# Sending the keys of a linear attention through a DRAM scratch and turning them in 32x32 blocks on VectorE

## The chip, the cores and the metric

The kernel runs on one core of a Trainium2 chip. The metric is the device time of one execution in microseconds, the median over several runs; less is better. Engine names are those of the profile: PE is TensorE (PEld its weight loads), DVE is VectorE, ACT is ScalarE, POOL is GpSimd, SP is SyncE, which here issues nearly all DMAs.

## The reference, cut to what matters

Input `x` is 16 images of 56 x 56 tokens with 128 channels, float32. Layer 0 is a group norm and shifted window attention with 4 heads over windows of 7 x 7 tokens, added to `x`. Layer 1 reads each image as 3136 tokens in order:

```
t = t + L1_attn(ln(t))    # causal linear attention, below
t = t + L1_ffn(ln(t))     # batch-normed projection, then a recurrence over all tokens

def L1_attn(x, W, b):                      # per image
    q, k, v = split(x @ W.T + b)
    q = elu(q) + 1;  k = elu(k) + 1
    num[t] = q[t] @ sum_{s <= t} outer(k[s], v[s])
    den[t] = q[t] . sum_{s <= t} k[s] + 1e-6
    return num / den
```

The change concerns `k = elu(k) + 1`, which the kernel calls the keys' features.

## The kernel before

All arithmetic is float32. An image's tokens are cut into six full groups of 512 tokens (four chunks of 128) and one short group of 64 tokens. A window row is 56 tokens x 7 rows, eight per image.

**The plan.** The work up to the recurrence is not written in program order. Every piece is a `plan.step(engine, cost, rank, emit, after, takes, drops, lag)`: its engine, how long it holds the engine, a due time, the function that issues it, the steps that must come first, the buffers it takes and those it drops, and after how long its result is there. `Plan.emit` runs a list schedule over all steps with these costs, repeats it forwards and backwards 200 times, keeps the shortest plan, and issues all steps in the order of their planned starts. So on each engine the order of instructions is fixed when the kernel is built. SP is planned like an engine: its steps are DMA issues, and it takes them in that order. The instructions that belong together of two images overlap in this order: while the window rows of one image are worked on, the token groups of the image before it are.

**A window row** (`window_row`): projections of queries and keys (L857) and values (L878) on PE, scores (L902), masking and maxima on DVE (L913, L925), subtraction on POOL (L928), exponential on ACT (L938), sums on DVE (L942), scaling on POOL (L947), a PE transpose (L957), and the mix with the values (L976), copied out by ACT.

**A token group** (`token_group`): output projection (L1224), added on DVE (L1233); statistics on DVE (L1080), the rest of the norm on POOL; the normalised tokens are turned so that channels lie on partitions (`xnT`). From `xnT` come two features, `feature(1)` for the keys (tile `f1`) and `feature(0)` for the queries (tile `f0`): a projection on PE (L1259), two activations on ACT (L1269, L1278) and a maximum on DVE (`larger`, L1287). Values come from L1312 and L1321. The products of keys and queries inside a chunk (L1375) are masked on DVE (L1385, tile `A`). `attend` adds up state times queries (L1404) and `A` times values (L1407); `gather` adds keys times values to the running state in `state_bank` (L1415), which ACT copies out per chunk (L1427). `gather` wants the keys with tokens on partitions (tile `k`), while `f1` has channels on partitions. DVE divides and updates the tokens (L1477, L1480, L1484), SP stores them to `x_d` (L1184), and a second norm and projection (L1502) gives the inputs of the recurrence (`staged`, stored by L1537, once per image).

**How something is turned.** There are two ways. On PE: four transposes of 128 x 128 into a PSUM bank and a copy by ACT; the keys take this way in all groups (`turn_k`, L1335, and `k_out`, L1339). Through DRAM (`through_dram`): SP stores the tile to a scratch (`away`, L1050), then issues four reads of 64 KB (`back`, L1057), which bring the 32-row blocks to the partitions where they belong, and one DVE instruction transposes within 32 x 32 blocks (L1129). The normalised tokens of both norms (keys `"a"` and `"f"` of `xn_d`) take this way in the full groups of images 0 to 14, as `blocks_moved` says; the last image and the short groups use PE. Four slots (`xp`) hold what is read back, three (`xm`) what is sent; `f1`, `f0`, `r`, `A` have one buffer each, `k` has two, PSUM has three banks (`b`) for everything but scores and states.

**DMA around it.** Besides, SP loads the tokens of later images by group (L323), loads each image a second time in 128-byte runs for the window attention (`load_blocks`, L335, turned by DVE in L676), and stores groups and staged inputs. All of these stand in one in-order queue.

After the plan comes the recurrence over the tokens, cut into segments (L1785, L1788, L1773, L1822, L1831), which the change does not touch.

Of the kernel before, what the change touches and what calls it, by code (L numbers as in the profile page):

```python
# [26 lines left out]


TOL2 = 2.0 ** -38
KEYS = ('f', 'a')  # L30


class Buf:
# [201 lines left out]
def tile_conv_attn_hybrid(  # L235
# [19 lines left out]
    nc = tc.nc  # L255
# [6 lines left out]
    G = 4  # L262
# [27 lines left out]
    xn_d = {  # L290
        key: dram.tile([B - 1, NG - 1, 4, P, P], F32, name=f"xn{key}_d") for key in KEYS
    }
# [65 lines left out]
    def flat(to):  # L358

        dims = " ".join("abc"[: len(to.shape) - 1])  # L360
        return to.rearrange(f"p {dims} -> p ({dims})")
# [66 lines left out]
    with ExitStack() as s1:  # L428
# [14 lines left out]
        def own(buf, *shape):  # L443

            key = buf.tag, buf.place
            if key not in owned:
                owned[key] = keep.tile(list(shape), F32, name=f"{buf.tag}_{buf.place}")
            return owned[key]
# [3 lines left out]
        def at_spare(buf):  # L452

            k = AT_SPARE[buf.tag] + buf.place
            return flat(spare[1])[:, GT * k : GT * (k + 1)]
# [109 lines left out]
        s = issued = plan.step("SP", 0.1, -1.0, lambda: None, lag=19.0)  # L565
# [80 lines left out]
        def part(g, full, mini):  # L646

            return full if g < NG - 1 else mini
# [392 lines left out]
        def blocks_moved(key, b, g):  # L1041

            return key in KEYS and b < B - 1 and g < NG - 1

        def through_dram(key, b, g, src, xp, rank, after, drops):

            there = xn_d[key][b, g]

            def away():
                nc.sync.dma_start(  # L1050
                    there.rearrange("s p r -> p s r"),
                    src().rearrange("p (s r) -> p s r", s=4),
                )

            def back():
                for s4 in range(4):
                    nc.sync.dma_start(  # L1057
                        at_spare(xp)[32 * s4 : 32 * (s4 + 1)].rearrange(
                            "i (q r) -> i q r", q=4
                        ),  # L1060
                        there[s4].rearrange("(q i) r -> i q r", q=4),
                    )

            s = plan.step("SP", 0.7, rank, away, after, drops=drops, lag=2.6)
            return plan.step("SP", 1.6, rank, back, [s], takes=[xp], lag=3.6)

        def layer_scale(t, g, d, key, rank, after, to, drops=()):
# [79 lines left out]
            if blocks:  # L1147
                s = through_dram(key, t["b"], g, lambda: d["xm"], xp, rank, [sc], [xn])
                s = plan.step(
                    "DVE",  # L1150
                    (0.59, 0.68),
                    rank,
                    turn_blocks,
                    [s, chain[key]],
                    takes=[to],
                    drops=[xp],
                )
                chain[key] = s
                return s, sc
# [40 lines left out]
        def token_group(b, g, i, t, turned_x, rows_done, oT_buf, xt_buf, rank):  # L1200


            n = f"{b}_{g}"
            d, df = {}, {}
# [3 lines left out]
            nt = t1 - t0  # L1208
# [38 lines left out]
            s = st("DVE", part(g, (0.61, 0.69), (0.20, 0.28)), rank, plus_attention, [s0, s1], drops=[bo])  # L1247
# [5 lines left out]
            def feature(j):  # L1253
                key = f"f{j}"
                bp, r, f = Buf("b"), Buf("r"), Buf(key)

                def proj():
                    d[f"p{j}"] = bank(bp, P, nt)
                    nc.tensor.matmul(  # L1259
                        d[f"p{j}"],  # L1260
                        awc_sb[:, j * P : (j + 1) * P],
                        d["xT"][:, :nt],
                        start=True,
                        stop=True,
                    )

                def relu():
                    d[f"r{j}"] = own(r, P, GT)[:, :nt]
                    nc.scalar.activation(  # L1269
                        d[f"r{j}"],  # L1270
                        d[f"p{j}"],
                        AF.Relu,
                        bias=bqk_neg[:, j : j + 1],
                        scale=-1.0,
                    )

                def expo():
                    nc.scalar.activation(d[f"r{j}"], d[f"r{j}"], AF.Exp, scale=-1.0)  # L1278

                def larger():  # L1280
                    d[key] = own(f, P, GT)
                    to, a1, a2 = d[key][:, :nt], d[f"p{j}"], d[f"r{j}"]
                    if j and blocks_moved("k", b, g):
                        to = to.rearrange("p (c k) -> p k c", k=G)
                        a1 = a1.rearrange("p (k c) -> p k c", k=G)
                        a2 = a2.rearrange("p (k c) -> p k c", k=G)
                    nc.vector.scalar_tensor_tensor(  # L1287
                        to,
                        a1,
                        bqk_one[:, j : j + 1],  # L1290
                        a2,
                        ALU.add,
                        ALU.max,
                    )

                p = st("PE", part(g, (0.86, 1.02), (0.17, 0.33)), rank, proj, [xo, *first], takes=[bp], drops=[xnT])
                s = st("ACT", part(g, (0.58, 0.69), (0.22, 0.31)), rank, relu, [p], takes=[r])
                s = st("ACT", part(g, (0.53, 0.63), (0.16, 0.26)), rank, expo, [s])
                return st("DVE", part(g, (0.65, 0.74), (0.18, 0.27)), rank, larger, [s], takes=[f], drops=[r, bp]), f

            first = [] if b else [made["awc"], made["bqk"], made["fwTc"]]
# [3 lines left out]
            def chunk(f, cc):  # L1305
                return f[:, CK * cc : CK * (cc + 1)]
# [22 lines left out]
            s = st("PE", part(g, (0.89, 1.05), (0.22, 0.38)), rank, values, [xo, *first, *last_pd[i % 2]], takes=[bv], drops=[xnT])  # L1329
# [10 lines left out]

            def turn_blocks():
                d["k"] = own(k, P, G, C)
                nc.vector.transpose(
                    d["k"].rearrange("p k (q c) -> p k q c", q=4),
                    at_spare(xp).rearrange("p (q c k) -> p k q c", q=4, k=G),
                )

            def keys(cc):
                if blocks_moved("k", b, g):
                    return d["f1"].rearrange("p (c k) -> p k c", k=G)[:, cc]  # L1350
                return chunk(d["f1"], cc)

            bk, k, bA, A = Buf("b"), Buf("k"), Buf("b"), Buf("A")
            if blocks_moved("k", b, g):
                xp = Buf("xp")
                s = through_dram("k", b, g, lambda: d["f1"], xp, rank, [fk], [bfk])
                ko = st(
                    "DVE",
                    (0.59, 0.68),
                    rank,  # L1360
                    turn_blocks,
                    [s, chain["k"]],
                    takes=[k],
                    drops=[xp],
                )
                chain["k"] = ko
            elif g < NG - 1:
                s = st("PE", (0.44, 0.61), rank, turn_k, [fk], takes=[bk], drops=[bfk])
                ko = st("ACT", (0.48, 0.59), rank, k_out, [s], takes=[k], drops=[bk])


            def products():
                d["pA"] = bank(bA, P, nk, np)
                for cc in range(nk):
                    nc.tensor.matmul(  # L1375
                        d["pA"][:, cc, :],
                        keys(cc),
                        chunk(d["f0"], cc)[:, :np],
                        start=True,
                        stop=True,  # L1380
                    )

            def A_out():
# [6 lines left out]
                )  # L1390

            s = st("PE", part(g, (0.89, 1.05), (0.13, 0.29)), rank, products, [fq, fk], takes=[bA], drops=[bfk])
            Ao = st("DVE", part(g, (0.60, 0.69), (0.13, 0.22)), rank, A_out, [s], takes=[A], drops=[bA])

# [98 lines left out]
            s = st("DVE", (0.29, 0.37), rank, divisors, pns)  # L1493
# [4 lines left out]
            s, scaled = layer_scale(t, g, df, "f", rank, [up], xfT, [xt_buf])  # L1498
# [24 lines left out]
            s = st("PE", part(g, (0.86, 1.02), (0.17, 0.33)), rank, whole, [s], takes=[bw], drops=[xfT])  # L1523
# [192 lines left out]
    with ExitStack() as s2:  # L1716
# [177 lines left out]
        d = ryo.tile([P, 2, B, SEG], F32, tag="y", name="seam")[:, 0, :, 0 : SEG - 1]  # L1894
# [95 lines left out]
```

## Time and profile before

| | before |
|---|---|
| median of 3 runs | 1694.72 us (1693.42 to 1697.08) |
| the profiled execution | 1699.48 us, span 1697.7 us |
| granted TensorE clock, mean | 0.992 |
| first to fifteenth store of staged inputs | 174.2 to 1480.6 us |
| HBM read, written | 147.94 MB, 122.65 MB |
| DMA queue that SP issues to | 537232 packets, 269.89 MB, 54.5% of 16 engines |

The profile shows one execution. A row of a group names line, engine, operation, output and inputs, shape and count, then total busy time, the mean of one in ns, and the engine's idle time just before with what ended it. The names in a row are the program's: tiles that lie in the buffer `spare` (all `xm` and `xp` slots do) are shown as `spare`; `xna_d` and `xnf_d` are the scratches of the two norms. A weight load and a matmul are recorded apart (PEld, PE), and a float32 matmul shows as two records. In a window row the columns are the stretch, its length, busy us with counts of PE, PEld, DVE, ACT and POOL, the granted clock, the DMA engines' busy share and GB/s.

### The profile page before, as it was taken

The page shows a single profiled execution, that of the slowest core. Times are in us where ns is not written, and L with a number is a line of the kernel's source. Part 1 is how long each engine was busy: PE and PEld are TensorE (multiplying, and loading weights), DVE is VectorE, ACT ScalarE, POOL GpSimd, SP SyncE. Part 2 cuts the span into 40 slices and gives each one's busy share as a digit, 9 for nine tenths or more (in the row PEclk, how much of TensorE's full clock was granted, in tenths as well). Part 3 has the DMA queues.
Part 4 walks back from the last instruction along what each step waited for, and adds up shares of the span by engine and source line. Part 5 has one row for each costly group of instructions (what it writes and reads, how often), then busy time and mean ns, then how long its engine had stood idle before and what let it go on. Part 6 is the DMA issues. An engine that isn't in the chain of part 4 may idle for free.

```text
span 1697.7 us, 63511 instructions
## 1 busy us (share of the span) xinstructions
PE 1651.5 (97%) x25819; PEld 1348.0 (79%) x25819; DVE 1444.7 (85%) x3354; ACT 1139.0 (67%) x2846; POOL 1152.5 (68%) x2042
## 2 busy tenths in 40 slices
PE   7999999999999999999999999999999998999997
PEld 6778878888887888888888888888787887786875
DVE  5889988898979898988988898989788876777997
ACT  5667667667676676766766767667666675666765
POOL 6788778688778687877876887787676765651000
PEclk9999999999999999999999999999999999999998
DMA  5465646364545547463746365545543343558999
GB/s 134 102 161 122 173 126 170 103 163 135 154 132 139 129 119 186 116 167 107 182 116 159 114 141 157 151 124 131 143 121 96 102 140 95 163 175 325 405 418 378
DMA packets 539117, 274.81 MB, mean 162 GB/s; under 512 B 208960, under 2 KB 522560, under 8 KB 537024
## 3 DMA queue, kind: packets, MB, share of 16 engines
q1 hardware_dynamic: 537232, 269.89, 54.5%
q8 instruction: 204, 3.34, 0.8%
q10 hardware_dynamic: 1584, 0.79, 0.2%
q14 instruction: 97, 0.79, 0.1%
HBM read 147.94 MB, written 122.65 MB: 159 GB/s over the span
## 4 chain that ended last, share of the span: by engine, by line
PE 81%; DVE 7%; POOL 4%; DMA 3%; issue 3%; SPq 1%; ACT 1%; DVEq 0%; POOLq 0%; ACTq 0%
PE bank L1259 9%; PE bank L857 9%; PE bank L878 6%; PE pair L902 6%; PE pair L957 5%; PE state_bank L1415 5%; PE pair L1404 5%; PE pair L1407 5%; PE pair L976 5%; PE bank L1312 5%; PE bank L1375 5%; PE bank L1224 5%; PE bank L1502 4%; DVE z_buf L1773 3%; PE z_buf L1785 3%
## 5 line engine op out<-in xcount | busy, mean ns | idle before, releaser
L928 POOL TENSOR_TENSOR s<-s,mx 128x784 f32<-128x784 f32 x128 | 192.4, 1503 | 84.9 <-DVE mx L925 82.3
L947 POOL TENSOR_TENSOR p_buf<-p_buf,rc 128x784 f32<-128x784 f32 x128 | 194.6, 1521 | 80.4 <-DVE rc L944 39.7
L1259 PE MATMUL bank<-xnT,awc_sb 128*128 128x512 f32 (+1 forms) x448 | 211.2, 554 | 4.6 <-DVE xt_buf L1233 3.4
L1269 ACT ACTIVATE r<-bank,bqk_neg 128x512 f32<-128x512 f32 (+1 forms) x224 | 142.7, 637 | 101.0 <-PE bank L1259 84.6
L1404 PEld LDWEIGHTS pair<-state,f 128*128 128x128 f32 x768 | 126.1, 191 | 53.5 <-issue 35.9
L1287 DVE SCALAR_TENSOR_TENSOR f<-bank,bqk_one,r 128x512 f32<-128x512 f32 (+1 forms) x224 | 147.6, 659 | 23.2 <-ACT r L1278 10.7
L1407 PE MATMUL pair<-v_buf,A 128*128 128x129 f32 x800 | 155.4, 276 | 0.8 <-issue 0.4
L967 ACT COPY pT<-pair 128x904 f32<-128x904 f32 x128 | 118.1, 923 | 54.6 <-PE pair L957 42.4
L1415 PEld LDWEIGHTS state_bank<-v_buf,k 128*128 128x128 f32 x768 | 123.7, 192 | 38.9 <-issue 21.0
L1415 PE MATMUL state_bank<-v_buf,k 128*128 128x129 f32 x768 | 153.8, 282 | 0.5 <-ACT state L1427 0.2
L1427 ACT COPY state<-state_bank 128x129 f32<-128x129 f32 x384 | 105.2, 274 | 72.7 <-PE state_bank L1415 69.9
L1404 PE MATMUL pair<-state,f 128*128 128x129 f32 x768 | 152.1, 280 | 0.0
L913 DVE TENSOR_TENSOR s<-pair,wmask_sb 128x784 f32<-128x784 f32 x128 | 122.9, 960 | 32.0 <-PE pair L902 27.8
L942 DVE TENSOR_REDUCE sm<-p_buf 128x16 f32<-128x784 f32 x128 | 121.9, 952 | 21.3 <-ACT p_buf L938 21.1
L1213 POOL TENSOR_TENSOR xt_buf<-xt_buf,bout_sb 128x512 f32<-128x512 f32 (+1 forms) x112 | 129.3, 1159 | 14.2 <-DMA xt_buf<-in_x_dram 13.9
L1788 ACT ACTIVATE y_a<-z_buf,bsh 128x256 f32<-128x256 f32 (+1 forms) x218 | 103.3, 474 | 45.5 <-PE z_buf L1785 41.5
L1278 ACT ACTIVATE r<-r 128x512 f32<-128x512 f32 (+1 forms) x224 | 130.7, 584 | 2.5
L902 PEld LDWEIGHTS pair<-kT,q_buf 32*49 32x49 f32 x8192 | 106.3, 121 | 32.3 <-issue 16.3
L1785 PE MATMUL z_buf<-y_a,fvT_sb 128*128 128x256 f32 (+1 forms) x432 | 129.7, 385 | 0.5 <-ACT y_a L1788 0.4
L902 PE MATMUL pair<-kT,q_buf 32*49 32x49 f32 x8192 | 122.6, 206 | 4.8 <-issue 4.8
L957 PEld LDWEIGHTS pair<-ident,p_buf 113*128 113x128 f32 x1024 | 108.1, 142 | 21.6 <-issue 9.6
L1407 PEld LDWEIGHTS pair<-v_buf,A 128*128 128x128 f32 x800 | 121.8, 192 | 3.9 <-issue 1.9
(162 smaller groups left out, 4619.0 us busy)
## 6 DMA issues: line engine op xcount, KB each, us to landing
x_d<-xt_buf SPq DMA_DIRECT2D x96, 256.0 KB, 2.5
xt_buf<-in_x_dram SPq DMA_DIRECT2D x93, 256.0 KB, 3.4
spare<-in_x_dram SPq DMA_DIRECT2D x60, 392.0 KB, 4.7
xs_d<-staged SPq DMA_DIRECT2D x15, 1568.0 KB, 7.0
xna_d<-spare SPq DMA_DIRECT2D x90, 256.0 KB, 2.5
spare<-xna_d SPq DMA_DIRECT2D x360, 64.0 KB, 2.0
xnf_d<-spare SPq DMA_DIRECT2D x90, 256.0 KB, 2.3
spare<-xnf_d SPq DMA_DIRECT2D x360, 64.0 KB, 2.1
```

Source lines behind the costliest of these rows:

```text
L857: nc.tensor.matmul(d[key], wqkv_sb[:, j * P : (j + 1) * P], xk, start=True, stop=True)
L902: nc.tensor.matmul(sc[64 * hh : 64 * hh + WT, hp, w * WT : (w + 1) * WT], qT[r : r + HD, w * WT : (w + 1) * WT], d["kT"][r : r + HD, w * W ...
L928: nc.gpsimd.tensor_tensor(d["sf"], d["sf"], d["mx"].unsqueeze(2).to_broadcast([P, nb, WT]), ALU.subtract,)
L947: nc.gpsimd.tensor_tensor(prf, prf, d["rc"].unsqueeze(2).to_broadcast([P, nb, WT]), ALU.mult)
L957: nc.tensor.transpose(pt[:, hp, w2, 0:NQ2], pr[0:NQ2, hp, 2 * w2 : 2 * w2 + 2, :].rearrange("p w k -> p (w k)"), ident[0:NQ2, 0:NQ2],)
L1259: nc.tensor.matmul(d[f"p{j}"], awc_sb[:, j * P : (j + 1) * P], d["xT"][:, :nt], start=True, stop=True,)
L1269: nc.scalar.activation(d[f"r{j}"], d[f"p{j}"], AF.Relu, bias=bqk_neg[:, j : j + 1], scale=-1.0,)
L1287: nc.vector.scalar_tensor_tensor(to, a1, bqk_one[:, j : j + 1], a2, ALU.add, ALU.max,)
L1404: nc.tensor.matmul(to, chunk(d["f0"], cc), t["states"][c], start=True, stop=False)
L1407: nc.tensor.matmul(to, d["A"][:, cc, :], v1[:, cc, :], start=c == 0, stop=True)
L1415: nc.tensor.matmul(t["pd"], d["k"][:, cc, :], v1[:, cc, :], start=c == 0, stop=True, skip_group_check=True,)
L1785: nc.tensor.matmul(z, fvT_sb, y_prev, start=False, stop=True, skip_group_check=True)
```

## The change

The keys join the tiles that go through DRAM: in the full groups of images 0 to 14, `f1` is stored to a scratch of its own, `xnk_d`, read back, and turned by DVE into `k`; `turn_k` and `k_out` stay for the last image. The way back differs from that of the norms. For the norms, POOL has already written its output with channels interleaved, and each of the four reads has four runs of 512 bytes per partition. `f1` is stored as it is, so each read picks, for each of 32 partitions, 16 runs of 32 elements (128 bytes). The planned costs of the two SP steps are those of the norms. A branch in `larger` and a helper `keys`, which interleaved the key features for such a way and were not entered before (`"k"` was not in `KEYS`), are taken out.

```diff
-KEYS = ('f', 'a')
+KEYS = ('f', 'a', 'k')
...
         def through_dram(key, b, g, src, xp, rank, after, drops):
             there = xn_d[key][b, g]
+            runs = there.rearrange("s (q i) r -> i (s q) r", q=4)
...
             def back():
                 for s4 in range(4):
-                    nc.sync.dma_start(
-                        at_spare(xp)[32 * s4 : 32 * (s4 + 1)].rearrange(
-                            "i (q r) -> i q r", q=4
-                        ),
-                        there[s4].rearrange("(q i) r -> i q r", q=4),
-                    )
+                    to = at_spare(xp)[32 * s4 : 32 * (s4 + 1)]
+                    if key == "k":
+                        to = to.rearrange("i (n c) -> i n c", c=32)
+                        part = runs[:, :, 32 * s4 : 32 * (s4 + 1)]
+                    else:
+                        to = to.rearrange("i (q r) -> i q r", q=4)
+                        part = there[s4].rearrange("(q i) r -> i q r", q=4)
+                    nc.sync.dma_start(to, part)
...
                 def larger():
                     d[key] = own(f, P, GT)
-                    to, a1, a2 = d[key][:, :nt], d[f"p{j}"], d[f"r{j}"]
-                    if j and blocks_moved("k", b, g):
...                                  # interleaved views of to, a1, a2
                     nc.vector.scalar_tensor_tensor(
-                        to, a1, bqk_one[:, j : j + 1], a2,
+                        d[key][:, :nt], d[f"p{j}"], bqk_one[:, j : j + 1], d[f"r{j}"],
...
             def turn_blocks():
                 d["k"] = own(k, P, G, C)
-                nc.vector.transpose(
-                    d["k"].rearrange("p k (q c) -> p k q c", q=4),
-                    at_spare(xp).rearrange("p (q c k) -> p k q c", q=4, k=G),
-                )
-            def keys(cc):
...
+                nc.vector.transpose(d["k"].rearrange("p k c -> p (k c)"), at_spare(xp))
...
             if blocks_moved("k", b, g):     # unchanged, entered now
                 xp = Buf("xp")
                 s = through_dram("k", b, g, lambda: d["f1"], xp, rank, [fk], [bfk])
                 ko = st("DVE", (0.59, 0.68), rank, turn_blocks, [s, chain["k"]],
                         takes=[k], drops=[xp])
```

More of the change, by code (lines that the diff above doesn't have):

```diff
@@ L1281, in larger @@
                     d[key] = own(f, P, GT)
-                    to, a1, a2 = d[key][:, :nt], d[f"p{j}"], d[f"r{j}"]
-                    if j and blocks_moved("k", b, g):
-                        to = to.rearrange("p (c k) -> p k c", k=G)
-                        a1 = a1.rearrange("p (k c) -> p k c", k=G)
-                        a2 = a2.rearrange("p (k c) -> p k c", k=G)
                     nc.vector.scalar_tensor_tensor(
-                        to,
-                        a1,
+                        d[key][:, :nt],
+                        d[f"p{j}"],
                         bqk_one[:, j : j + 1],
-                        a2,
+                        d[f"r{j}"],
                         ALU.add,
@@ L1342, in turn_blocks @@
                 d["k"] = own(k, P, G, C)
-                nc.vector.transpose(
-                    d["k"].rearrange("p k (q c) -> p k q c", q=4),
-                    at_spare(xp).rearrange("p (q c k) -> p k q c", q=4, k=G),
-                )
-            def keys(cc):
-                if blocks_moved("k", b, g):
-                    return d["f1"].rearrange("p (c k) -> p k c", k=G)[:, cc]
-                return chunk(d["f1"], cc)
+                nc.vector.transpose(d["k"].rearrange("p k c -> p (k c)"), at_spare(xp))
             bk, k, bA, A = Buf("b"), Buf("k"), Buf("b"), Buf("A")
@@ L1376, in products @@
                         d["pA"][:, cc, :],
-                        keys(cc),
+                        chunk(d["f1"], cc),
                         chunk(d["f0"], cc)[:, :np],
```

## The prediction

> **What bounds the kernel now.** I read the whole-span page first, then the busy time cut into images, then TensorE's list of instructions in order of time, then who waits for whom, then the DMA views. The span has three parts: a start of 175 us (the first image), thirteen images of 93.3 us each from 174.6 to 1388 us (the stores of the staged inputs stand 93.3 us apart: first at 174.2, fifteenth at 1480.6), then the last two images and the recurrence at the end. The change touches images 0 to 14, six groups each: 90 groups.
>
> ```profile
> PE 1651.5 (97%) x25819; PEld 1348.0 (79%) x25819; DVE 1444.7 (85%) x3354; ACT 1139.0 (67%) x2846; POOL 1152.5 (68%) x2042
> ...
> 174.60:1388.00 1213.40, 1205.17 (x20156) 989.62 (x20155) 1057.09 (x2539) 829.15 (x2113) 921.90 (x1619) 1.00 0.51 137
> ```
>
> The second row is the thirteen images: length, then busy PE, PEld, DVE, ACT, POOL, the granted clock and the DMA share. PE is busy 1205 of 1213 us, so per image 92.7 of 93.3; DVE 81.3. Busy PE is not yet PE at its limit, since each piece's end is modelled. So I read starts, which are not:
>
> ```profile
> 550.36 1.02 PE L1259 MATMUL bank<-xnT,awc_sb 128*128 128x512 f32 x2
> 551.22 0.94 PE L957 MATMUL pair<-ident,p_buf 113*128 113x113 f32 x8
> 551.99 0.60 PE L1335 MATMUL bank<-ident,f 128*128 128x128 f32 x4
> 552.43 1.06 PE L1224 MATMUL bank<-wout_sb,oT_buf 128*128 128x128 f32 x8
> ```
>
> Four transposes of the keys (L1335) hold PE from 551.99 to 552.43, 0.44 us; their 0.60 us runs on under the next line. Adding an image's instructions by such distances (a window row 4.65 us, a full group 8.3, the short group 1.9) gives 8 x 4.65 + 6 x 8.3 + 1.9 = 89 us of 93.3: PE is filled to 95%, and it waits for nobody for long:
>
> ```profile
> PE pair L902 <- issue: 3.0, 1, 3.0
> PE pair L957 <- POOL p_buf L947: 0.8, 1, 0.8
> ```
>
> These are PE's two largest waits in the whole stretch 100 to 1200 us. So the order of work is bound by PE, with DVE 12 us per image behind it.
>
> A rule here speaks against this reading. The Trainium skill (Trainium Kernel Development and Optimization, Best Practices) holds matmul busy time a bad measure of how near TensorE is to its limit and asks for the weight loads' busy share; by that share, 989.6 of 1213.4 or 82%, PE would have 17 us of room per image, the relief would buy nothing and the time would stay near 1695. The starts above decide for me: by them the sum below holds.
>
> **The change, part by part.**
>
> *Removed from PE:* 90 x 4 transposes, 90 x 0.44 = 39.6 us, or 2.64 us per image. *Removed from ACT:* 90 copies (L1339, 590 ns), 53 us; ACT is busy 64 of 93 us, so nothing. The PSUM bank held meanwhile, about 2.1 us per group (551.99 to the copy's end at 554.11), becomes free: not counted.
>
> *Added on DVE:* 90 block transposes of 128x512. The nearest rows have the same size and engine:
>
> ```profile
> L1129 DVE STREAM_TRANSPOSE xfT<-spare 128x512 f32<-128x512 f32 x90 | 63.2, 702 | 26.6 <-DMA spare<-xnf_d 24.2 <-PE pair L976 2.2
> L1129 DVE STREAM_TRANSPOSE xnT<-spare 128x512 f32<-128x512 f32 x90 | 63.2, 702 | 14.8 <-DMA spare<-xna_d 12.3 <-PE bank L1259 2.0
> L1335 PE MATMUL bank<-ident,f 128*128 128x128 f32 x384 | 58.5, 274 | 1.9 <-issue 1.9
> L1339 ACT COPY k<-bank 128x512 f32<-128x512 f32 x96 | 56.7, 590 | 25.0 <-PE bank L1335 24.5
> ```
>
> 90 x 0.702 = 63 us, 4.2 per image: DVE goes from 81.3 to 85.5 us. The new PE time of an image is at best 93.3 - 2.6 = 90.7. So DVE has 5.2 us left per image, where it had 12. `larger()` and the products' operand keep their shape: the branch taken out of them was never entered with these keys.
>
> *Added on SP and the DMA queue:* per group one write of 256 KB and four reads of 64 KB. The write has a twin (away of `f`, `a`). The reads are in runs of 128 bytes, 512 each, where the twins have 128 runs of 512 bytes. Their price lies between the twin and the image load, which has 128-byte runs too, but 3136 of them:
>
> ```profile
> spare<-in_x_dram SPq DMA_DIRECT2D x60, 392.0 KB, 4.7
> ...
> xna_d<-spare SPq DMA_DIRECT2D x90, 256.0 KB, 2.5
> spare<-xna_d SPq DMA_DIRECT2D x360, 64.0 KB, 2.0
> ...
> 533.50:534.00 0.50, 0.50 (x5) 0.26 (x4) 0.50 (x2) 0.50 (x2) 0.50 (x1) 1.00 1.07 375
> 537.50:538.00 0.50, 0.50 (x7) 0.50 (x6) 0.50 (x2) 0.31 (x3) 0.50 (x2) 1.00 1.38 217
> ```
>
> The last two rows are half microseconds in which the queue is full, of the staged store (long runs, 375 GB/s) and of an image load (128-byte runs, 217 GB/s; last column). So a 64 KB read costs the engines 0.30 us instead of 0.17, and a group 256 KB / 375 GB/s + 4 x 0.30 = 1.9 us. That is 11 us of an image in which the queue is now half idle (share 0.51): hidden. The landing goes by runs from 2.0 towards 4.7 us; interpolated, 2.0 + 2.7 x 384 / 3008 = 2.3.
>
> The Trainium skill (DMA: Bandwidth & Descriptors, Specifications) puts line rate at 512 bytes and more; 217 against 375 GB/s agrees in kind. By the rule the short runs count against the change; by the rows they cost 4 x 0.13 us of a half idle queue per group, and nothing in the sum.
>
> *The way round.* The keys are now ready after: write 2.5, issue of three reads 3 x 0.43, last landing 2.3 = 6.1 us (bounds 5.8 with landing 2.0, 8.7 with 4.7 and 0.50 per issue), against 0.44 on PE and 0.59 on ACT before. What covers it is what the planner puts between. I took the built program's order on DVE and added trace durations from the maximum that makes `f1` to the block transpose that turns it: mean 8.7 us, smallest 5.0. At 6.1 us, 10 of 90 groups lack cover, 4.5 us in all; at 8.7, 48 groups and 72 us. I take the first, the nearer row by number of runs.
>
> *Waits added.* On DVE the new transpose may wait for its data, with every mask, sum and statistic behind it. The twins wait 24.2 and 12.3 us in 90 each. I give the keys the worse, 24 us or 1.6 per image (from 4.5, the cover alone, to 72). On SP each read waits for its write:
>
> ```profile
> SPq L1057 <- DMA xna_d<-spare: 122.2, 65, 8.5
> SPq L1057 <- DMA xnf_d<-spare: 88.8, 65, 4.8
> ```
>
> About 1.2 us per group; with the issues, 0.38 + 4 x 0.43, a group costs SP 3.3 us, 20 per image. Behind it stand the stores of `x_d`, the loads of x and the reads of `a` and `f`. SP has the time, but the twins may come later.
>
> *The sum, per image.* PE 90.7. DVE 85.5 + 1.6 (keys) + 2.4 (twins, 36.5 / 15) = 89.5. PE still ends last, by 1.2 us. With the two so near, part of DVE's new waits reaches PE: I take a third of 24, 8 us. The first image, where PE is not filled, has the way round uncovered once or so: 3 us (0 to 6). So -39.6 + 8 + 3 = -28.6. The profiled execution is 1699.5 us (span 1697.7), which makes 1670.9; it stands 4.8 above the median of the runs, so the median becomes 1666.
>
> **The rivals.**
>
> *PE is relieved, nothing lost:* -39.6, 1655. For it: PE hardly waits today. It is the end of the forecast's case.
>
> *DVE takes over as the bound, about even.* 93.3 is reached when DVE's waits grow by 3.8 us per image beyond my 89.5, 0.6 us per key turn. Then the median lies within 3 us of 1695. For it: DVE already waits 32 us for scores and 29 for values, which PE hides only while DVE has slack. Against: those waits are the other side of a full PE.
>
> *SP's queue makes all block turns late, slower.* One in-order queue now has 18 round trips per image instead of 12. The 180 turns wait 36.5 us now, 0.20 each. The image is longer than 93.3 once 18 turns wait (93.3 - 85.5) / 18 = 0.43 us each. At 0.55 it is 95.4 us, +2.1 x 15 = +32: 1726. For it: in the built order 23 of 90 key reads stand directly behind their write, and only 5 of the `f` reads still do, against 8; SP waits there already 211 us. Against: SP has idle time, and the planner charges 0.7 + 1.6 us for these steps and orders by it.
>
> *The change does not do what it says:* excluded, the built program has 360 PE transposes fewer, 90 DVE transposes and 450 DMAs more.
>
> **How the numbers follow.** Forecast with its own range 1655 to 1684: 0.72. Between there and no change, DVE taking most of it: 0.10, of which 0.05 still shows as faster. Slower by SP's queue or DVE: 0.18, mostly by little. The range reaches from just under the full relief, 1652, to 1698, over the even case. A measurement here tells about 0.2%, 3.4 us, from no change. Faster 0.77, same 0.06, slower 0.17.
>
> **What would show it.** The keys' PE transposes 24 instead of 384, PE about 1612 us busy, an image 91.5 us by the staged stores. DVE about 1508 us, the key turn near 0.70 us with 24 us of DMA waits (over 72 refutes the cover). The key read landing at 2.3 us. `xnf` and `xna` turns waiting 24 and 12 us, not double. Wrong: images of 93 us or more with PE waiting on DVE tiles (`f`, `A`, `v_buf`), or turns waiting over 0.43 us each.

## The result, and the profile after

The changed kernel takes 1741.43 us (median of 4 runs, 1730.20 to 1742.71) against 1694.51 us: ratio 1.026, interval 1.0216 to 1.0304. It is slower, where 1666 was forecast. The profiled execution has 1742.71 us (span 1740.9 us).

The page of the changed kernel first: the busy rows, and the chain of work that ended last by engine and by line.

```profile
PE 1642.2 (94%) x25459; PEld 1318.2 (76%) x25459; DVE 1488.7 (86%) x3444; ACT 1100.0 (63%) x2756; POOL 1148.4 (66%) x2042
...
PE 29%; DMA 23%; DVE 23%; SPq 11%; POOL 7%; issue 5%; ACT 1%; DVEq 0%; POOLq 0%
SPq L1065 10%; DMA xnk_d<-f 7%; DMA spare<-xnk_d 5%; PE bank L1262 3%; PE bank L857 3%; DMA xnf_d<-spare 3%; DMA xna_d<-spare 3%; DMA spare<-xnf_d 2%; DVE f L1285 2%; PE z_buf L1775 2%; DVE sm L942 2%; PE bank L878 2%; PE bank L1365 2%; PE bank L1492 2%; PE state_bank L1405 2%
```

Before, the chain was nearly all PE:

```profile
PE 81%; DVE 7%; POOL 4%; DMA 3%; issue 3%; SPq 1%; ACT 1%; DVEq 0%; POOLq 0%; ACTq 0%
```

Now PE has 29% of it, and the front of the list is the issue of the reads from DRAM (L1065), the write of the keys and their reads. The transposes are gone from PE (360 records fewer) and are on DVE (90 more), as the change says; SP and the DMAs, 4% of the chain before, are 34% of it now.

Where does the time go? The last token update of an image, on its short group, is a good mark: it stands at 164.7 us for the first image and 1455.2 for the fifteenth before the change, and at 160.5 and 1497.2 after it. So the first image is not slower. The next fourteen take 95.5 us each instead of 92.2, and that is all: the last image takes 72.5 us instead of 73.1, the recurrence 171.2 instead of 169.4. The two stretches of fourteen images as windows, before and after (length; busy PE, PEld, DVE, ACT, POOL; granted clock; DMA share; GB/s):

```profile
164.70:1455.20 1290.50, 1276.99 (x21324) 1048.05 (x21323) 1116.87 (x2688) 878.13 (x2239) 972.85 (x1719) 0.99 0.51 136
```

```profile
160.50:1497.20 1336.70, 1276.52 (x21300) 1027.65 (x21299) 1167.12 (x2794) 851.19 (x2176) 979.01 (x1739) 0.99 0.66 165
```

PE was idle for 13.5 us in the first and is idle for 60.2 us in the second. Its busy time is the same in both, though 37 us of transposes (84 groups of 0.44 us) are gone from the second: the matmuls that stay are recorded longer or overlap less, so the idle time is not all that PE lost. PE's largest wait is now for the turned keys, and who keeps DVE from turning them is seen in what DVE waits for (total us, times, longest), changed kernel:

```profile
PE state_bank L1405 <- DVE k L1341: 22.7, 17, 5.4
...
DVE k L1341 <- DMA spare<-xnk_d: 74.7, 53, 7.1
DVE xfT L1132 <- DMA spare<-xnf_d: 22.1, 21, 2.6
DVE xnT L1132 <- DMA spare<-xna_d: 18.2, 19, 2.3
```

Of 90 key turns 53 find no data, and DVE stands still with everything behind them. The reads of the two norms (24.2 and 12.3 us before) are hardly later than they were. The longest such stop in full, SP's list of the changed kernel and then DVE's, in order of time (start, length, line, what):

```profile
488.35 0.43 SPq L1051 DMA_DIRECT2D xna_d<-spare  x1
488.82 0.51 SPq L335 DMA_DIRECT2D spare<-in_x_dram  x1
492.88 1.81 SPq L1065 DMA_DIRECT2D spare<-xna_d  x4
495.09 0.38 SPq L1051 DMA_DIRECT2D xnk_d<-f  x1
495.51 0.50 SPq L1187 DMA_DIRECT2D x_d<-xt_buf  x1
496.06 0.53 SPq L1051 DMA_DIRECT2D xna_d<-spare  x1
498.83 1.92 SPq L1065 DMA_DIRECT2D spare<-xnk_d  x4
```

```profile
490.29 0.73 DVE L1285 SCALAR_TENSOR_TENSOR f<-bank,bqk_one,r 128x512 f32<-128x512 f32 x1
...
497.00 0.29 DVE L771 BATCH_NORM_AGGREGATE mv<-gst 128x2 f32<-128x42 f32 x1
504.45 0.71 DVE L1341 STREAM_TRANSPOSE k<-spare 128x512 f32<-128x512 f32 x1 [7.15 <-DMA spare<-xnk_d]
```

The keys' features are ready at 491.02. SP is then standing in front of the reads of `a`, whose write (issued at 488.35, an image load of 392 KB behind it) lands only at 492.88. Those reads take SP to 494.7; the keys' write goes out at 495.09, 4.1 us late; their reads start at 498.83, when it has landed; the data is there at 504.3, 3.6 us after the last of them was issued, where the forecast has 1.9. DVE had reached the key turn at 497.3. The Trainium skill (DMA: Bandwidth & Descriptors, Anatomy of one DMA) says that DMA engines do not wait on semaphores, and that any such wait is made by the issuing sequencer ahead of the dispatch; the rows show what it means here: 3.5 us of standing still at 489.3, paid by a transfer that had nothing to do with it.

Over all 90 groups the means of the changed kernel's trace are:

| part of the way round, us | forecast | measured, mean |
|---|---|---|
| features ready to write issued | 0 | 1.2 |
| write issued to first read issued | 2.5 | 3.4 |
| four reads issued | 1.7 | 2.5 |
| last issue to landing | 1.9 | 1.8 (median landing 2.3 less 0.49) |
| sum | 6.1 | 8.9 |

The transfers themselves are near the forecast by their medians (group rows of the DMA issues, changed kernel; the last number is the median from issue to landing):

```profile
xna_d<-spare SPq DMA_DIRECT2D x90, 256.0 KB, 2.8
spare<-xna_d SPq DMA_DIRECT2D x360, 64.0 KB, 2.1
xnk_d<-f SPq DMA_DIRECT2D x90, 256.0 KB, 2.7
spare<-xnk_d SPq DMA_DIRECT2D x360, 64.0 KB, 2.3
```

So the 2.8 us beyond the forecast are mostly the line before the transfers. The write stands in it for 1.2 us. Another 0.9 us pass until the first read is issued, about half of it because the write lands later on the mean (3.0 us over the 52 landings that are recorded, 2.5 in the forecast). The four issues take 0.8 us more: 0.49 us each instead of 0.43, and longer in some groups.

### The profile page after: what moved, and what is told of

The parts are those of the page before. It is cut to its first block, busy times and chain, and to the rows that moved or that the text cites. A ratio compares the mean times of both kernels' runs of the same rounds, so it can differ in the third digit from the quotient of the medians.

```text
span 1740.9 us, 63539 instructions
## 1 busy us (share of the span) xinstructions
PE 1642.2 (94%) x25459; PEld 1318.2 (76%) x25459; DVE 1488.7 (86%) x3444; ACT 1100.0 (63%) x2756; POOL 1148.4 (66%) x2042
## 3 DMA queue, kind: packets, MB, share of 16 engines
q1 hardware_dynamic: 774832, 317.10, 66.5%
## 4 chain that ended last, share of the span: by engine, by line
PE 29%; DMA 23%; DVE 23%; SPq 11%; POOL 7%; issue 5%; ACT 1%; DVEq 0%; POOLq 0%
SPq L1065 10%; DMA xnk_d<-f 7%; DMA spare<-xnk_d 5%; PE bank L1262 3%; PE bank L857 3%; DMA xnf_d<-spare 3%; DMA xna_d<-spare 3%; DMA spare<-xnf_d 2%; DVE f L1285 2%; PE z_buf L1775 2%; DVE sm L942 2%; PE bank L878 2%; PE bank L1365 2%; PE bank L1492 2%; PE state_bank L1405 2%
## 5 line engine op out<-in xcount | busy, mean ns | idle before, releaser
L1262 PE MATMUL bank<-xnT,awc_sb 128*128 128x512 f32 (+1 forms) x448 | 217.0, 568 | 6.9 <-DVE v_buf L1319 1.9
L1405 PE MATMUL state_bank<-v_buf,k 128*128 128x129 f32 x768 | 158.0, 288 | 25.9 <-DVE k L1341 22.7
L938 ACT ACTIVATE p_buf<-s 128x784 f32<-128x784 f32 x128 | 112.4, 879 | 31.9 <-POOL s L928 31.7
L1365 PEld LDWEIGHTS bank<-f,f 128*128 128x128 f32 x800 | 105.0, 197 | 31.2 <-DVE f L1285 12.8
L1341 DVE STREAM_TRANSPOSE k<-spare 128x512 f32<-128x512 f32 x90 | 63.6, 707 | 75.2 <-DMA spare<-xnk_d 74.7
```

Source lines behind the costliest of these rows:

```text
L1262: nc.tensor.matmul(d[f"p{j}"], awc_sb[:, j * P : (j + 1) * P], d["xT"][:, :nt], start=True, stop=True,)
L1365: nc.tensor.matmul(d["pA"][:, cc, :], chunk(d["f1"], cc), chunk(d["f0"], cc)[:, :np], start=True, stop=True,)
L1405: nc.tensor.matmul(t["pd"], d["k"][:, cc, :], v1[:, cc, :], start=c == 0, stop=True, skip_group_check=True,)
```

## The experiments

Three theories were put against each other at first. A: the way round is longer than the order allows for, and the order is fixed, so DVE stops. B: 90 more transposes are too much for DVE, however early the data. C: 450 more DMA issues and 47 MB more traffic delay everybody. Times are medians, ratios are to the kernel before in the same session.

### One part at a time

**DVE's work alone** (`e4_dve_alone`), the kernel before with

```diff
+                if b < B - 1:   # turns f1 into a tile that nobody reads
+                    st("DVE", (0.59, 0.68), rank, turn_extra, [fk], drops=[bfk])
```

> The kernel before, keys turned on PE as ever, with 90 more block transposes of 128x512 on DVE, from the key features into a tile that nobody reads. Theory A: DVE has the slack, 1694-1703. Theory B: the extra 63 us of DVE make the order longer, 1715-1745. Theory C: 1694-1700.

Measured: 1709.71 us, 1.0072 (1.005 to 1.0094). DVE is busy 1490.6 us, as in the changed kernel. So the work alone costs some 12 us: more than A expected, less than B. The figure is rough, since this is a new order too, and a new order alone moves the kernel before by some 5 us (below). It is not the 47.

**The DMAs alone** (`e5_dma_alone`), the changed kernel with the keys turned on PE as before and the DRAM way made for nobody:

```diff
-                s = through_dram("k", ...)
-                ko = st("DVE", (0.59, 0.68), rank, turn_blocks, [s, chain["k"]], ...)
...
-            elif g < NG - 1:
+                through_dram("k", ...)     # drops its own slot
+            if g < NG - 1:                 # turn_k and k_out stay
```

> The kernel before, keys turned on PE as ever, with the changed kernel's DMAs beside it: each group's key features are written to the scratch and read back in the same four reads, which nobody uses. Theory A: 1695-1705, the queue has room. Theory B: 1694-1700. Theory C: 1715-1745, with DVE waiting longer for the reads of the two norms (over 60 us, 36 before).

Measured: 1786.32 us, 1.0521 (1.0497 to 1.0545), slower than the change itself. Nobody waits for the keys here, but the norms' reads are late:

```profile
DVE xfT L1133 <- DMA spare<-xnf_d: 73.4, 35, 7.3
DVE xnT L1133 <- DMA spare<-xna_d: 62.0, 32, 5.0
```

So C, not A as I had put it: in an order planned with these figures the load on SP and the queue is enough, and it need not be the keys that are late. The next two runs divide it. Both have the order of `e5_dma_alone` on every engine.

**Few bytes** (`f1_dma_tiny`):

```diff
                 if key == "k":
+                    to, part = to[:, 0, 0:32], part[:, 0, 0:32]          # write: 128 runs
...
-                        part = runs[:, :, 32 * s4 : 32 * (s4 + 1)]
+                        to, part = to[:, 0], runs[:, 0, 0:32]            # read: 32 runs
```

> The kernel with the DMAs alone (keys turned on PE, written and read back for nobody), in the very same order on every engine and with the same waits, but each of the keys' five DMAs carries little: 128 runs of 128 bytes out, 32 runs of 128 bytes per read back, 32 KB per group instead of 512. Theory C1, SP's queue (450 more issues and waits in one in-order queue make the norms' reads late): time stays at 1760-1790, DVE's waits for the norms' reads above 100 us. Theory C2, traffic (the DMA engines are busier and every landing later): time falls to 1695-1720, those waits to 35-60 us.

**No waits** (`f2_dma_no_waits`):

```diff
+                if key == "k":
+                    part = ident.unsqueeze(1).to_broadcast([P, 4, P])    # write a constant
...
+            runs = x[b].rearrange("h w c -> (h w) c")[t0:t1].rearrange(...)  # read the input
```

> The kernel with the DMAs alone, again in the very same order and with the full bytes, but the keys' write sends a constant tile and the keys' reads fetch the input x, so none of the five waits for DVE or for a landing. C1 by waits (SP stands still for the key maximum and the write's landing, about 113 us by the trace): time falls to 1700-1730. C1 by issue time alone (450 x 0.45 us = 200 us of SP): stays at 1760-1790. C2, traffic: stays at 1760-1790.

Measured: 1743.61 us (1.0266, 1.0247 to 1.0284) and 1760.49 us (1.0369, 1.0335 to 1.0403). Taking the bytes away gains 43 us, taking the waits away 26, and neither brings the time back. Both parts of C are real: in an order without room, the bytes cost time and so do the stops of SP. DVE's waits of the run with few bytes:

```profile
DVE xfT L1134 <- DMA spare<-xnf_d: 56.9, 37, 4.7
DVE xnT L1134 <- DMA spare<-xna_d: 38.7, 26, 5.2
```

The 45 us that still separate it from the kernel before are issue time, waits and an order made for these steps, not divided further.

**Short runs** (`e2_runs512`), the changed kernel in its own order, the keys read in the norms' four runs of 512 bytes per partition, which puts them in a wrong arrangement:

```diff
-                    if key == "k":
+                    if key == "none":
```

> The changed kernel in the very same order, with the keys read back in the norms' runs of 512 bytes (4 per partition) instead of 128 bytes (16). The keys arrive in a wrong arrangement. If the short runs are what makes the reads late, the time falls to 1700-1720 and DVE's wait for the keys from 75 us to under 40. If the way round is long for other reasons (SP's line, landings of the write), it stays at 1730-1745: by the landing of the reads, 2.3 us against 2.1, and their issue, 0.49 against 0.43 us, the short runs can be 0.4 us of the 9.

Measured: 1727.62 us, 1.018 (1.0149 to 1.0211), DVE's wait for the keys 54.6 us instead of 74.7. The runs of 128 bytes cost 14 us in this order, in the gap between the edges of the two expectations (1720 and 1730): 0.2 us more of landing and 0.06 more per issue, times four, count where there is no room.

**No wait for the write** (`e3_no_round_trip`):

```diff
-            runs = there.rearrange(...)
+            runs = xn_d[key][max(b - 1, 0), g].rearrange(...)
...
+                ready = [*after, aways[b - 1, g]] if b else [s]
+                return plan.step("SP", 1.6, rank, back, ready, takes=[xp], lag=3.6)
```

> The changed kernel, but the four reads fetch the keys that the image before has stored (image 0 its own), so they wait for the new keys' maximum on DVE and for no write; the write is still made. Every instruction, DMA and byte stays; only the wait for the landing of the write is gone from the way of the keys, and the planner knows it. The attention uses keys of the wrong image. Theory A: the way round falls from 9 to 5-6 us and is covered, DVE waits for it under 30 us, time 1665-1705. Theory B: 1725-1745, since DVE has the same work. Theory C: 1725-1745, since SP and the queue have the same work.

Measured: 1736.62 us, 1.0226 (1.0193 to 1.0258). A miss for A: the way is shorter by a whole transfer and the time is the same. DVE still waits 57.5 us for the keys. The planner was told of the shorter way and allowed that much less time: by the trace the reads have landed 5.7 us after the features instead of 8.9 (means), and DVE comes to the turn after 6.6 us instead of 9.6. This turned the question round: not how long the way is, but how much longer than the plan has it.

### The plan's figures

The order comes from planned figures: a result is there 2.6 us after a write's start and 3.6 us after that of the reads, which hold SP for 1.6 us. The trace has 3.4 us to the next issue, about 4.3 to the reads' landing (2.5 + 1.8), and 2.1 (median) to 2.5 us of SP.

**The keys' figures as measured, with some room** (`e1_long_lag`):

```diff
+            if key == "k":
+                s = plan.step("SP", 0.7, rank, away, after, drops=drops, lag=3.6)
+                return plan.step("SP", 2.1, rank, back, [s], takes=[xp], lag=5.4)
```

> The changed kernel, with the planner told a longer way round for the keys: lag 3.6 us for the write (was 2.6), 5.4 us and 2.1 us of SP for the reads (were 3.6 and 1.6), as the changed kernel's trace has them; nothing else is edited, the planner makes a new order from it. Theory A, late keys (the way round takes 9 us where the order covers about 6.3, and DVE stands still in order until the data is there): DVE's wait for the keys' reads falls from 75 us to under 25 and the time from 1741 to 1680-1715. Theory B, DVE load (90 more block transposes are too much for DVE, however early the data): the waits fall, the time stays at 1725-1745. Theory C, DMA and SP load (47 MB more, 450 issues more delay everybody else): the waits for the keys move to other readers, the time stays at 1725-1745.

Measured: 1714.43 us, 1.01 (1.0077 to 1.0123). The keys are waited for 15.2 us instead of 74.7, but now the reads of `f` for 51.1 instead of 22.1. The time is just inside A's range, but the wait has moved to a neighbour, which was C's sign.

**The same for all three tiles** (`h1_all_lags`):

```diff
-            s = plan.step("SP", 0.7, rank, away, after, drops=drops, lag=2.6)
-            return plan.step("SP", 1.6, rank, back, [s], takes=[xp], lag=3.6)
+            s = plan.step("SP", 0.7, rank, away, after, drops=drops, lag=3.6)
+            return plan.step("SP", 2.1, rank, back, [s], takes=[xp], lag=5.4)
```

> The changed kernel with the planner told the longer way round for all three tiles that go through DRAM: lag 3.6 us for each write, 2.1 us of SP and lag 5.4 us for each set of reads. If late data in a fixed order is what costs (A, or C1 through its effect on all three), DVE's waits for the three kinds of reads fall from 90 us (with the longer lag for the keys alone) to under 50 and the time from 1714 to 1675-1705. If the load itself costs, whatever the order allows for, it stays at 1705-1730.

Measured: 1660.64 us, 0.9782 (0.9756 to 0.9807): faster than both kernels, below the range that was expected, with the same instructions, bytes and DMAs as the changed kernel. Its page and then DVE's waits:

```profile
PE 1612.4 (97%) x25458; PEld 1305.6 (79%) x25459; DVE 1486.6 (90%) x3444; ACT 1091.5 (66%) x2756; POOL 1151.7 (70%) x2042
...
q1 hardware_dynamic: 774832, 317.10, 69.9%
...
PE 72%; DVE 10%; DMA 7%; POOL 4%; SPq 3%; issue 3%; ACT 1%; DVEq 0%; POOLq 0%; ACTq 0%
```

```profile
DVE k L1341 <- DMA spare<-xnk_d: 12.7, 12, 2.2
...
DVE xnT L1132 <- DMA spare<-xna_d: 2.7, 2, 1.8
DVE xfT L1132 <- DMA spare<-xnf_d: 0.7, 1, 0.7
```

PE carries the chain again (72%). The queue is fuller (69.9% of 16 engines, 66.5% in the changed kernel), and the way round is longer: by the four parts of the table above it is 10.1 us here, 8.9 in the changed kernel. But it is covered. From the end of the features to the start of the turn 11.9 us pass on the mean, of which DVE is idle for 1.1, so 10.8 us of its work lie between the two. In the changed kernel it is 9.6 us with 1.8 of idle time, so 7.8 us of work for a way of 8.9.

**The kernel before with the same figures** (`h0_before_lags`): the same diff on the kernel before.

> The kernel before, with the same longer lags for its two tiles that go through DRAM (3.6 us for the write, 2.1 us of SP and 5.4 us for the reads). If the gain of the run with all lags longer (1661) comes of the change, with a plan that knows what it costs, this one stays near the kernel before, 1685-1700, since its DVE waited only 36 us for these reads. If the gain comes of the better plan alone, it falls to 1655-1670 too, and the change is worth nothing.

Measured: 1683.82 us, 0.991 (0.9888 to 0.9933). DVE no longer waits for these reads at all (36.5 us before). So the better figures are worth 11 to 15 us without the change, just more than expected, and the change is worth 1683.8 - 1660.6 = 23 us with them.

**Which figure?** (`h3_lags_only`, `h4_cost_only`): the two halves.

```diff
+            s = plan.step("SP", 0.7, rank, away, after, drops=drops, lag=3.6)          # h3
+            return plan.step("SP", 1.6, rank, back, [s], takes=[xp], lag=5.4)
...
+            s = plan.step("SP", 0.7, rank, away, after, drops=drops, lag=2.6)          # h4
+            return plan.step("SP", 2.1, rank, back, [s], takes=[xp], lag=3.6)
```

> The changed kernel with the longer lags (3.6 and 5.4 us) for all three tiles, but SP's planned time for the reads left at 1.6 us. If what was missing is the latency that the order allows for, it is as good as with both edits: 1655-1675, DVE waiting under 30 us for the reads. If SP was planned too full (1.6 us for what holds it 2.1), it stays at 1690-1741.

> The other half: SP's planned time for the reads 2.1 us, the lags as they were (2.6 and 3.6 us). If the latency is what was missing, it stays at 1715-1745 with DVE waiting over 80 us. If SP's line was the cause, it falls to 1655-1680.

| changed kernel, us | SP 1.6 us for the reads | SP 2.1 us |
|---|---|---|
| lags 2.6 and 3.6 us | 1741.4 | 1706.9 |
| lags 3.6 and 5.4 us | 1678.9 | 1660.6 |

The lags take 62 us (with 2.1 us of SP, 46), SP's holding time 34 (with the longer lags, 18). Neither half reaches the whole. The first is just behind what was expected of it, with 45 us of waits instead of under 30; the second lies between its two expectations. Each cell is an order of its own, and two orders with the short lags can differ by 28 us (below), so the part of SP's holding time is less sure than that of the lags.

**Longer still** (`h2_longer_lags`): 4.0 and 6.0 us.

> The changed kernel with still longer lags (4.0 us for each write, 6.0 us for the reads). If waits for late data still cost something at 1661 (13 us of DVE's for the keys were left), it falls to 1650-1660. If the cover is bought with buffers held longer, it stays or rises, 1660-1680.

Measured: 1664.08 us, 0.9794 (0.9772 to 0.9816). DVE waits only 7 us for the reads in all, and nothing more is gained. These two orders with long lags lie 3 us apart. Whether more buffers would do the same as better figures was not tried: the four slots `xp` serve three kinds of tiles now instead of two.

### How much is chance

The planner keeps the best of 200 passes, so any edit gives another order. Two runs change nothing but a setting of the planner, how far ahead its passes look (us):

```diff
-    AHEAD = (30.0, 20.0, 10.0, 5.0)
+    AHEAD = (28.0, 18.0, 9.0, 4.0)
```

> The changed kernel with other looks ahead in the planner (28, 18, 9, 4 instead of 30, 20, 10, 5), its costs and lags as they are: how much of 1741 is this one order. If the order is just unlucky, this one lies far from it, under 1715. If the short lags are the cause, it stays within 15 us of 1741, with DVE waiting 80-130 us for the three kinds of reads.

> The kernel before with other looks ahead in the planner (28, 18, 9, 4), nothing else: how far a new order alone moves it. If orders with the short lags differ by chance as much as the two of the changed kernel did (28 us), this one lies 10 us or more from the kernel before, on either side. If the kernel before is not sensitive, since DVE has slack for its waits, within 6 us of it.

Measured: the changed kernel 1769.50 us (1.0424, 1.0381 to 1.0467), 28 us slower than with its own order; the kernel before 1702.37 us (1.0035, 1.0018 to 1.0052). So nothing shows 1741 to be an unlucky order: the one other is slower, and the kernel before moved by 5 us only. For the changed kernel, a difference of less than some 30 us between two orders with short lags is not to be read as the effect of an edit; the 27 us of `e1_long_lag` and the 5 us of `e3_no_round_trip` are of that size. The 80 us from 1741 to 1661 are beyond it, and they come with the waits: the runs of the changed kernel, by what DVE waits for its three kinds of reads (times are medians; waits and clock are those of the profiled execution).

| run | DVE's wait for reads, us | time, us | granted clock |
|---|---|---|---|
| h2_longer_lags | 7 | 1664.1 | 0.996 |
| h1_all_lags | 17 | 1660.6 | 0.997 |
| h3_lags_only | 45 | 1678.9 | 0.996 |
| h4_cost_only | 83 | 1706.9 | 0.994 |
| e1_long_lag | 92 | 1714.4 | 0.991 |
| e2_runs512 | 97 | 1727.6 | 0.989 |
| e3_no_round_trip | 114 | 1736.6 | 0.986 |
| changed kernel | 115 | 1741.4 | 0.987 |
| e6_other_plan | 141 | 1769.5 | 0.983 |

From the first to the last row 134 us of waiting go with 105 us of time: of a microsecond that DVE stands still, about 0.8 arrive at the end. This is a slope over nine orders, which differ in other things too, and no measurement of a single stop.

### Another queue

**The keys' DMAs from ACT** (`g1_act_queue`):

```diff
+            queue = nc.scalar if key == "k" else nc.sync
...
+                s = plan.step("ACT", 0.5, rank, away, after, drops=drops, lag=2.8)
+                return plan.step("ACT", 2.0, rank, back, [s], takes=[xp], lag=4.2)
```

> The changed kernel with the keys' write and reads issued from ACT's queue (planned there: 0.5 us and lag 2.8, 2.0 us and lag 4.2) and the norms' left on SP. C1: SP is as before the change, the norms' reads are waited for under 45 us together, and the time falls to 1670-1710 unless ACT, 1100 us busy and with some 200 us of issues added, stands in the way. C2 or B: 1725-1745.

Measured: 1973.01 us, 1.161 (1.1571 to 1.1649). ACT does stand in the way, far more than expected. Its copies now wait behind the keys' reads in its own line, and with them the running state:

```profile
ACT state L1421 <- DMA spare<-xnk_d: 30.6, 8, 8.4
ACT kT L871 <- DMA spare<-xnk_d: 23.1, 8, 4.7
ACT p_buf L938 <- DMA spare<-xnk_d: 15.8, 4, 4.9
```

The norms' reads on SP, relieved, were waited for longer than before (`f`: 97.7 us). Why the whole is 275 us was not settled; the rows account for a part.

## Why the prediction was wrong, step by step

**The first step that failed is the way round.** The prediction has 6.1 us, bounds 5.8 and 8.7, from landings and issues alone, with SP free whenever it is wanted. It measured 8.9 on the mean, above the upper bound. Part of the difference stood in the trace of the kernel before: from a twin's write to its first read 3.1 to 3.3 us pass there on the mean, not 2.5, and from that issue to the last landing 4.0 to 4.2, so that a twin's way was 7.1 to 7.5 us before any load was added. The prediction named 3.3 us of SP per key group and 18 round trips in one line, and put none of it into the way.

The cover was nearer, but not right. Its 8.7 us add the durations of DVE's instructions, and neighbouring records overlap (the features' record ends at 491.02 in the stop above, the next begins at 490.95). From starts, as the prediction reads PE, the changed kernel has 7.8 us of DVE's work between features and turn. With this cover a way of 6.1 us leaves 13 groups uncovered by 9 us in all, and a way of 8.9 us leaves 69 by 122; the same list by durations gives 43 and 62. The trace has 53 waits and 74.7 us. So the way decides, and comparing it with the cover gives the size of the waits, not each of them.

**The keys' wait** of 24 us, with 72 named as what would refute the cover, measured 74.7. Taking the twins' wait as a model was the mistake: theirs is what is left where the planner allows 2.6 and 3.6 us for ways of 7.1 to 7.5 us, and the keys' way, 1.2 us to the write and 7.7 from there, is longer for the same allowance.

**The second step that failed is the share of DVE's waits that reaches PE,** a third in the prediction. DVE's waits rose from 36.5 to 115.0 us, by 78.5, and the kernel is 47 us slower than before where PE was relieved of 39.6: 86 us are lost, more than the whole rise, so other losses are in it that were not divided. Between the orders of the changed kernel the share is about 0.8. A third does hold in the kernel before, where 36.5 us of waits were worth 11 to 15. The reason was in the prediction: DVE 12 us per image behind PE before the change, 1.2 after it by its sum. With that little between two engines, a stop of one is nearly a stop of both.

Neither step alone explains the miss. In the prediction's own sum, a rise of 78.5 us passed on by a third makes 1684, and its 24 us passed on in full make 1682; 78.5 us passed on in full make 1737.

**The DMA queue hides the traffic:** not in this order. Landings grew little (write of `a` 2.5 to 2.8 us), and yet the bytes were worth 43 us where the order had no room (few bytes against full bytes). In the order with room they were hidden, at a fuller queue.

**Right:** PE as the bound and its relief, once DVE hardly waits (1612 us busy was forecast; 1642.2 is found in the changed kernel, 1612.4 with the longer figures; the change is worth 23 us between the two kernels with these figures, of 28.6 forecast). That nearness is in part luck: the forecast's 8 us of passed-on waits and 3 us of the first image are not shown to be what is missing there. Right also are the length of a transpose (707 ns, 63.6 us in all) and the landing of the short reads (2.3 us). DVE's busy time was forecast at 1508 us and is 1488.7: it rose by 44, again because records overlap. The first image was not 3 us slower but 4 faster.

**The rivals.** "SP's queue makes all block turns late" named the place and the sign. Its turning point, 0.43 us per turn, is what the trace has (115.0 / 270 = 0.43), and there the kernel is already 47 us slower, not even. It had the twins late; they were not (36.5 us of waits before, 40.3 after), the keys were, until a plan gave the keys more room and `f` paid. Its chance, 0.18 with all that ends slower, was too low: "the planner charges for these steps and orders by it" was taken as a point against it, when the charges were the weak point.

## What to carry to other kernels

An order fixed at build time is as good as the latencies it was built with. Here they were too short before the change already, and fell further short after it: adding transfers to the in-order queue made the round trips through it longer, the neighbours' too (write to first read 3.1 to 3.3 us before, 3.7 after). So measure issue to use, not issue to landing, put that into the plan, and judge the change only then. Compare the way round, with its queueing in it, with the work that the built order puts between producer and consumer, and add that work up from starts. And ask how much slack is left between the two fullest engines: here a third of the waits arrived at the end with 12 us of slack per image, and most of them with about 1 us.

The version to keep is the change with the longer figures: 1660.64 us, 0.978 (0.9756 to 0.9807) of the kernel before.

## What the runs showed of the hardware

- In half a microsecond of full DMA engines, an image load in runs of 128 bytes moved 217 GB/s, where the staged store in long runs moved 375 (kernel before). A 64 KB read in 512 such runs lands only 0.2 us later than one in 128 runs of 512 bytes (2.3 and 2.1 us). In `e2_runs512` and the changed kernel, the same order, the short runs cost 14 us.
- A queue with 69.9% of 16 engines busy goes with the fastest kernel here, one with 66.5% with a kernel 80 us slower. The busy share said nothing on whether transfers were late.
- In the runs of the changed kernel the granted TensorE clock is lower where DVE stops more: 0.996 to 0.997 with up to 45 us of waits, 0.983 at 141, 0.948 in the run from ACT's queue. The kernel before has 0.992 at 36 us, so the relation is loose. Three runs of the changed kernel at 0.987 took 1741 to 1743 us, the one at 0.992 took 1730. Just behind the stop shown above the clock is 0.50 from 504.0 to 510.8 us, where it was 1.00 from 490 on. Whether the gaps cause it was not tested. The product of span and missing clock is 22.6 us in the changed kernel (1740.9 x 0.013) and 5.0 in the fastest (1656.5 x 0.003); by this estimate it can be up to 18 of the 80 us between them.
